# Making VectorE's order by hand in the first stage of a four-layer graph network, with an earlier adjacency load and GpSimd additions cut into tiles

## The chip, the cores and the metric

The kernel runs on one core of one Trainium2 chip. The metric is device time in microseconds (us) of one execution. Times of the kernel before: 2691.99, 2691.94, 2691.20, 2691.12 and 2691.70 us, median 2691.7. One further execution was recorded by the hardware profiler.

## What is computed

Input x is 128 graphs of 64 nodes with 256 features, float32; adj is one 64x64 matrix for all graphs. Four layers follow each other; each ends with a layer norm over the features of x plus the layer's output.

```python
# layer 0: three products with (adj * adj), weights 256->512->1024->256
h = relu(einsum('nm,bmh->bnh', adj*adj, x @ W1))
h = relu(einsum('nm,bmh->bnh', adj*adj, h @ W2))
x = layernorm(x + einsum('nm,bmh->bnh', adj*adj, h @ W3))
# layer 1: features turned into the eigenvectors U of the normalised Laplacian
deg = sum(A, 0) + sum(A, 1) - diagonal(A)
_, U = eigh(rsqrt(deg)[:, None] * (diag(deg) - A) * rsqrt(deg)[None, :])
x = layernorm(x + U @ (relu((U.T @ x) @ W1 + b1) @ W2 + b2))
# layer 2: two graph convolutions, then LSTMs over windows of 1, 2, 3, 4 nodes
x = layernorm(x + lstm_windows(relu(adj @ (relu(adj @ (x @ Wg0 + bg0)) @ Wg1 + bg1))))
# layer 3: attention with the graph as a mask
h = x @ W + b_lin
s = einsum('bnd,bmd->bnm', h, h) * adj
x = layernorm(x + softmax(where(s == 0, -1e16, s)) @ h + b)
```

## The kernel before

The 8192 rows of x lie in SBUF as the tile X, 64 tiles of 128 rows (two graphs each) by 256. The adjacency stands twice on the diagonal of a 128x128 tile (ad2), so that one product mixes two graphs. Its transpose is adT2, the transposed square sqT2.

**First stage (up to about 983 us of the profiled execution).** Two things run at once:

- layer0(g), for 32 steps g, each a pair of row tiles: products with sqT2, W1, W2 and W3 (lines 590-630). A step ends with one 128x512 product (L628, seen in the profile as ps<-s,sqT), the residual addition on VectorE (L629) and rows_norm (L444): statistics on VectorE (L452, L453), reciprocal root on GpSimd (L454, L455), application on VectorE (L457). Two steps are in flight at a time.
- eigen (L40-433), one long generator that computes U for the 64x64 matrix: setup (L84-124), 62 Householder reflectors (L135-178), a tridiagonal stage (L181-267), six bisection passes (L272-291), two recurrences (L300-307), eigenvectors and their signs (to L433). Nearly all of it is small VectorE work; a few products and square roots go to TensorE and ScalarE.

All TensorE products write PSUM tiles from one pool of five (psa, tag "ps"), each released when its reader has read it.

**The order of work.** The functions are generators. Each `yield` hands over a due time on a planned clock now[0], in us, that advances by a fixed cost per product (L580). In eigen, after(n, turns) adds 0.21 us for each of n VectorE operations and 0.6 for each turn over ScalarE, and returns that time plus 0.3. The loop at L638-654 always goes on with the first stream that is due, eigen ahead of the steps. In the block `tc.manual_schedule(engines={PE})` the TensorE queue takes exactly the order in which the loop issues; the order of VectorE, ScalarE, GpSimd and of the DMA queues is made by the framework's own scheduler from its estimates. Every engine works through its queue in order: an instruction that waits holds all behind it.

In one reflector (L135-178) VectorE computes the norm of the rest of a row (L142-145), ScalarE its root (L146), VectorE the reflection vector v (L147-152); TensorE multiplies v and a unit vector with AQ (L156, L157); VectorE then makes the scalars (L158-170), the next row (L172, L173) and the updates of AQ (L174-177).

**Loads.** SP's queue loads W1, the two diagonal blocks of ad2, W2, X tiles 2-3, W3, the rest of X, then smaller weights. ScalarE's queue loads X tiles 0 and 1, a64 (the adjacency for eigen) and eig_c (seven 64x64 constant matrices, the identity among them). GpSimd's queue loads four bias rows broadcast to all partitions (wide).

**Second stage.** Layers 1 to 3 run for 16 groups of four row tiles, three groups in flight, with TensorE's order again made by the loop (L930-946) from due times such as CELL, the time from the last product of an LSTM step to its state (by the number of columns: 256, 168 or 128). GpSimd adds bias rows to X in layer 1 (L721) and layer 3 (L863), each in one instruction over 128x1024, and reorders the LSTM output (L840). The recurrent products appear as ps<-hs,whh, the input products as ps<-w,wih, and layer 1's product with the eigenvectors as ps<-ut,v.

Of the kernel before, what the change touches and what calls it, by code (L numbers as in the profile page):

```python
# [15 lines left out]
N = 64  # L16
# [23 lines left out]
def eigen(tc, stack, a, cst, u2, ut2, now):  # L40
# [25 lines left out]
    eye = cst[:, CONSTS.index("eye"), :]  # L66
# [17 lines left out]
    yield 4.0  # L84
# [22 lines left out]
    dl = sb([N, 1], "c6")  # L107
    V.tensor_sub(dl, deg, dia)
    m = sb([N, N], "m")
    V.tensor_scalar(m, s2, -0.5, None, op0=ALU.mult)  # L110
    V.tensor_mul(m, m, C["off"])
    V.scalar_tensor_tensor(m, C["eye"], dl, m, op0=ALU.mult, op1=ALU.add)
# [21 lines left out]
    after(1)  # L134
    for i in range(N - 2):  # L135
# [10 lines left out]
        S.activation(sq, ss, AF.Sqrt)  # L146
        V.tensor_scalar(g0, rest, 0.0, -1.0, op0=ALU.is_gt, op1=ALU.mult)  # L147
# [6 lines left out]
        yield after(21, 0.5)  # L154
# [19 lines left out]
        V.scalar_tensor_tensor(qt, vt, c2, pt, op0=ALU.mult, op1=ALU.add)  # L174
        V.scalar_tensor_tensor(AQ[:, 0, j:], qr[:, j:], vt, AQ[:, 0, j:], op0=ALU.mult, op1=ALU.add)
        V.scalar_tensor_tensor(AQ[:, 0, j:], xr[:, j:], qt, AQ[:, 0, j:], op0=ALU.mult, op1=ALU.add)
        V.scalar_tensor_tensor(AQ[:, 1, :], pq[:, 1, :], vt, AQ[:, 1, :], op0=ALU.mult, op1=ALU.add)
        xr = nx

# [264 lines left out]
def rows_norm(tc, pool, x, half):  # L444

    nc = tc.nc
    n = x.shape[1]
    st = pool.tile([P, n, 6], F32, name="ln_st")
    mv = pool.tile([P, n, 2], F32, name="ln_mv")
    rs = pool.tile([P, n], F32, name="ln_rs")  # L450
    for t in range(n):
        nc.vector.bn_stats(st[:, t, :], x[:, t, :])  # L452
        nc.vector.bn_aggr(mv[:, t, :], st[:, t, :])  # L453
    nc.gpsimd.tensor_scalar(rs, mv[:, :, 1], EPS, None, op0=ALU.add)  # L454
    nc.gpsimd.tensor_tensor(rs, rs, half[:, :n], ALU.pow)  # L455
    for t in range(n):
        nc.vector.tensor_scalar(x[:, t, :], x[:, t, :], mv[:, t, 0:1], rs[:, t:t + 1],  # L457
                                op0=ALU.subtract, op1=ALU.mult)


@with_exitstack
def kernel(
# [57 lines left out]
    for h in range(2):  # L520
        hs = slice(h * N, (h + 1) * N)
        nc.sync.dma_start(ad2[hs, hs], adj)
    for t in range(2):
        nc.scalar.dma_start(X[:, t, :], x_t[:, t, :])
    aw1 = load(wa, "aw1", a_w1, "(k p) f -> p k f", [P, 2, 512], p=P)
    nc.scalar.dma_start(a64, adj)
    nc.scalar.dma_start(eig_c, consts)
# [4 lines left out]
    nc.sync.dma_start(X[:, 2:4, :], x_t[:, 2:4, :])  # L532
    aw3 = load(wa, "aw3", a_w3, "(k p) f -> p k f", [P, 8, D], p=P)
    for t in range(4, NT, 2):
        nc.sync.dma_start(X[:, t:t + 2, :], x_t[:, t:t + 2, :])
    for h in range(2):
        nc.sync.dma_start(adst[h * N:(h + 1) * N, :], adj)
# [23 lines left out]
    for name, src in (("b_b1", b_b1), ("b_b2", b_b2), ("c_b0", c_b0), ("d_b", d_b)):  # L561
        wide[name] = keep.tile([P, src.shape[0]], F32, name=f"wide_{name}")
        nc.gpsimd.dma_start(wide[name], src.partition_broadcast(P))
# [5 lines left out]

    pt = tl(psa, [P, 512], "ps")  # L570
    PE.transpose(pt[:, :P], ad2, ident)
    V.tensor_copy(adT2, pt[:, :P])
    V.tensor_mul(sqT2, adT2, adT2)
# [16 lines left out]
    def layer0(g):  # L590
# [37 lines left out]
        mm(p, sqT2, s3)  # L628
        V.tensor_add(xs, p, xs)  # L629
        rows_norm(tc, small, xs, half)  # L630

    todo = [layer0(g) for g in range(NT // 2)]
    eig = [0.0, eigen(tc, phase_a, a64, eig_c, u2, ut2, now)]
    going = []
    with tc.manual_schedule(engines={mybir.EngineType.PE}):
# [45 lines left out]
    CELL = {256: 2.6, 168: 2.2, 128: 1.9}  # L683
# [35 lines left out]
    def layer1(xs):  # L719
        a = yield from mixed(xs, u2, (now[0], now[0]))  # L720
        nc.gpsimd.tensor_tensor(xs, xs, ub2.unsqueeze(1).to_broadcast([P, 4, D]), ALU.add)  # L721
# [131 lines left out]
    def layer3(xs, g, ready):  # L853
# [9 lines left out]
        nc.gpsimd.tensor_tensor(xs, xs, wide["d_b"].unsqueeze(1).to_broadcast([P, 4, D]), ALU.add)  # L863
# [125 lines left out]
```

## Time and profile before

| | |
|---|---|
| median of five executions | 2691.7 us |
| the profiled execution | 2691.99 us, its span 2690.2 us |
| granted TensorE clock, mean | 0.985 |
| TensorE products, busy | 2585.8 us (96%) |
| TensorE weight loads, busy | 2260.6 us (84%) |
| VectorE / ScalarE / GpSimd, busy | 1345.2 / 1030.0 / 240.5 us |
| first product of layer 0 | starts at 9.51 us |
| last product of the first stage's steps | starts at 982.24 us |
| reflectors, first and last product read (L166) | 37.8 and 391.5 us |
| bisection passes, first and last start (L276) | 408.3 and 622.7 us |
| end of eigen | 792 us |
| one group of the second stage, in its middle | 103.45 us |

The span runs from the first to the last instruction. A busy row counts the time in which an engine had an instruction in execution. "Idle before" and "waits" name, for the time in which an engine had nothing to do, the instruction whose end let it go on; they are inferred from semaphore events. PSUM tiles are named ps in all lines, so a wait of TensorE for "DVE X L629" is a wait until that addition has read its tile. A float32 product shows as two matmul instructions, so counts are twice those of the code. The granted clock is TensorE's, 1.00 or 0.50 of full speed in this trace.

### The profile page before, as it was taken

The numbers are of one execution on the slowest core, as the hardware profiler recorded it, in microseconds if no ns is written. First come the engines' busy times: TensorE is split into PE (matmuls) and PEld (weight loads), VectorE is DVE, ScalarE is ACT, GpSimd is POOL, SyncE is SP. The second block draws the span as 40 slices with busy tenths as digits, with TensorE's granted clock in tenths as the row PEclk, the third lists the DMA queues.
The fourth block names the chain that finished last, engine by engine and source line by source line (L and its number), as shares of the span: only waits on it lengthen the run. The fifth ranks groups of instructions, "written<-read, shape, count | busy, mean of one in ns | idle before, by whom it ended". The sixth has DMA issues, their size and how long they took to land.

```text
span 2690.2 us, 39840 instructions
## 1 busy us (share of the span) xinstructions
PE 2585.8 (96%) x15384; PEld 2260.6 (84%) x15384; DVE 1345.2 (50%) x5277; ACT 1030.0 (38%) x2526; POOL 240.5 (9%) x336
## 2 busy tenths in 40 slices
PE   7999999999999999999999999999999999999995
PEld 5888887777788887998898898998998988978993
DVE  4777768888510123335445445444444444453345
ACT  2222222222222224454544544445445444445442
POOL 0000000000000010102101101101101011010002
PEclk9999999999999999999999999999999999999997
DMA  8000000000000010000000000000000000000000
GB/s 270 1 1 1 1 1 1 1 1 1 1 1 0 0 48 0 1 9 9 1 9 9 1 9 9 1 9 9 1 9 9 1 9 9 1 9 1 1 1 24
DMA packets 24414, 32.19 MB, mean 12 GB/s; under 512 B 2352, under 2 KB 21040, under 8 KB 24224
## 3 DMA queue, kind: packets, MB, share of 16 engines
q1 hardware_dynamic: 23536, 28.68, 3.2%
q8 instruction: 121, 1.98, 0.3%
q0 software_dynamic: 176, 0.46, 0.1%
q10 hardware_dynamic: 512, 0.51, 0.1%
q14 instruction: 69, 0.57, 0.1%
HBM read 21.25 MB, written 8.39 MB: 11 GB/s over the span
## 4 chain that ended last, share of the span: by engine, by line
PE 50%; DVE 3%; ACT 2%; POOL 1%; issue 1%; POOLq 0%; DVEq 0%; ACTq 0%
PE ps L579 48%; PE ps L686 1%; DVE X L457 1%; POOL ln_rs L455 1%; DVE ln_st L452 1%; DVE X L848 1%; ACT gates L785 1%; PE ps L877 1%; ACT L785 0%; ACT L890 0%; ACT att L890 0%; POOL ln_rs L454 0%; DVE ln_mv L453 0%; DVE hs L795 0%; DVE X L915 0%
## 5 line engine op out<-in xcount | busy, mean ns | idle before, releaser
L579 PE MATMUL ps<-w,wih 128*128 128x128 f32 (+2 forms) x4992 | 891.1, 319 | 1.5 <-ACT w L587 0.7
L579 PEld LDWEIGHTS ps<-w,wih 128*128 128x128 f32 x4992 | 763.1, 191 | 49.3 <-issue 7.2
L785 ACT ACTIVATE gates<-ps,cbi 128x128 f32<-128x128 f32 (+2 forms) x1248 | 499.1, 409 | 533.2 <-PE ps L579 524.7
L579 PE MATMUL ps<-hs,whh 128*128 128x128 f32 (+2 forms) x3072 | 540.5, 303 | 14.3 <-DVE hs L795 14.3
L579 PEld LDWEIGHTS ps<-hs,whh 128*128 128x128 f32 x3072 | 452.3, 191 | 42.2 <-DVE hs L795 19.0
L579 PE MATMUL ps<-m,aw 128*128 128x256 f32 x2048 | 457.0, 381 | 4.7 <-DVE X L629 4.7
L579 PEld LDWEIGHTS ps<-m,aw 128*128 128x128 f32 x2048 | 386.9, 191 | 67.1 <-issue 11.0
L587 ACT ACTIVATE h<-ps 128x256 f32<-128x256 f32 (+1 forms) x320 | 136.2, 426 | 446.4 <-PE ps L579 446.4
L579 PE MATMUL ps<-aw,h 128*128 128x256 f32 x1024 | 229.4, 380 | 0.0
L579 PEld LDWEIGHTS ps<-aw,h 128*128 128x128 f32 x1024 | 193.1, 190 | 36.7 <-issue 12.2
L790 DVE TENSOR_TENSOR gates<-gates 128x256 f32<-128x256 f32 (+2 forms) x256 | 89.8, 351 | 211.5 <-ACT gates L785 211.3
L454 POOL TENSOR_SCALAR ln_rs<-ln_mv 128x2 f32<-128x2 f32 x128 | 31.1, 243 | 1486.5 <-DVE ln_mv L453 1284.3
L457 DVE TENSOR_SCALAR X<-X,ln_mv,ln_rs 128x256 f32<-128x256 f32 x256 | 104.2, 448 | 108.9 <-POOL ln_rs L455 108.9
L793 ACT ACTIVATE gates<-c 128x128 f32<-128x128 f32 (+2 forms) x288 | 98.1, 341 | 106.8 <-DVE c L792 92.5
L804 DVE TENSOR_TENSOR w<-gates 128x256 f32<-128x256 f32 (+2 forms) x160 | 73.9, 467 | 126.5 <-PE ps L579 81.5
L579 PE MATMUL ps<-aw,m 128*128 128x512 f32 x256 | 127.6, 622 | 0.0
L629 DVE TENSOR_TENSOR X<-ps,X 128x512 f32<-128x512 f32 x32 | 21.6, 676 | 208.7 <-PE ps L579 208.7
L789 DVE TENSOR_TENSOR c<-c,gates 128x128 f32<-128x128 f32 (+2 forms) x192 | 65.6, 342 | 113.0 <-ACT gates L785 111.1
L795 DVE TENSOR_TENSOR hs<-gates 128x128 f32<-128x128 f32 (+2 forms) x192 | 63.5, 331 | 95.4 <-ACT gates L793 74.8
L840 POOL COPY w<-w 128x512 f32<-128x512 f32 x32 | 35.6, 1112 | 791.1 <-DVE w L804 791.1
L598 ACT COPY m<-ps 128x256 f32<-128x256 f32 x192 | 71.3, 373 | 71.2 <-PE ps L579 62.6
L280 DVE RECIPROCAL br<-Q 64x16 f32<-64x16 f32 x378 | 92.4, 244 | 12.4
(325 smaller groups left out, 2693.0 us busy)
## 6 DMA issues: line engine op xcount, KB each, us to landing
out_dram<-X SPq DMA_DIRECT2D x32, 256.0 KB, 2.1
X<-in_x_dram SPq DMA_DIRECT2D x31, 256.0 KB, 6.0
wih<-in_c_ih_dram SPq DMA_DIRECT2D x4, 1024.0 KB, 8.0
aw<-in_a_w_dram SPq DMA_DIRECT2D x3, 1024.0 KB, 12.3
whh<-in_c_hh_dram SPq DMA_DIRECT2D x3, 1024.0 KB, 5.3
aw<-in_a_w_dram SPq DMA_DIRECT2D x1, 512.0 KB, 4.7
cw<-in_c_w_dram SPq DMA_DIRECT2D x2, 256.0 KB, 4.4
X<-in_x_dram ACTq DMA_DIRECT2D x2, 128.0 KB, 4.1
```

The lines of the kernel that those rows point to most:

```text
L280: V.reciprocal(r, Q[:, k - 1, :])
L457: nc.vector.tensor_scalar(x[:, t, :], x[:, t, :], mv[:, t, 0:1], rs[:, t:t + 1], op0=ALU.subtract, op1=ALU.mult)
L579: PE.matmul(out, lhsT, rhs, start=start, stop=stop)
L587: S.activation(dst, src, AF.Relu)
L598: S.copy(dst[:, c, :], p[:, :2 * P])
L785: S.activation(gate[q][:, h, :], pp, AF.Tanh if q == "g" else AF.Sigmoid, bias=bias[:, j:j + 1])
L789: V.tensor_mul(c[:, h, :], c[:, h, :], gate["f"][:, h, :])
L790: V.tensor_mul(to, gate["i"][:, h, :], gate["g"][:, h, :])
L793: S.activation(gate["i"][:, h, :], c[:, h, :] if p > 1 else to, AF.Tanh)
L795: V.tensor_mul(new[:, h, :], gate["o"][:, h, :], gate["i"][:, h, :])
L804: V.tensor_mul(hT[:, h, slice(first + p - 1, first + nw * p, p), :], gate["o"][:, h, :].rearrange("p (w b) -> p w b", b=8), gate["i"][:, h ...
L840: nc.gpsimd.tensor_copy(as3(hb[:, k, :], 8), hT[:, k, :, :].rearrange("p n b -> p b n"))
```

## The change

1. In the first stage VectorE's queue follows the loop too: `manual_schedule` names PE and DVE, and the transpose of ad2 with the making of adT2 and sqT2 stands inside the block.
2. rows_norm becomes a generator norm_parts in two parts, with a `yield` between GpSimd's reciprocal root and VectorE's application. In layer0 the addition follows 0.4 us of planned time after its product, the application 3.5 us after the statistics.
3. In a reflector the updates of AQ are kept in a list and issued in the next reflector, after its square root has been issued. The due time of the next product is after(20) instead of after(21, 0.5).
4. In eigen's setup the diagonal is no longer taken out of m by a mask: deg takes the place of dl. The identity comes from the tile ident instead of the loaded constants, and eigen's first due time is 2.0 instead of 4.0.
5. The adjacency is loaded first, on ScalarE's queue; X tiles 0 and 1 move to SP's, X tiles 2-3 ahead of W2; eig_c moves behind X, and the broadcast bias rows move from GpSimd's queue to SP's.
6. GpSimd's two additions are issued as four instructions over 128x256.
7. CELL for 256 columns is 3.3 instead of 2.6.

```diff
@@ eigen, setup
-    dl = sb([N, 1], "c6")
-    V.tensor_sub(dl, deg, dia)
     m = sb([N, N], "m")
     V.tensor_scalar(m, s2, -0.5, None, op0=ALU.mult)
-    V.tensor_mul(m, m, C["off"])
-    V.scalar_tensor_tensor(m, C["eye"], dl, m, op0=ALU.mult, op1=ALU.add)
+    V.scalar_tensor_tensor(m, C["eye"], deg, m, op0=ALU.mult, op1=ALU.add)
@@ eigen, reflectors
+    late = []
     for i in range(N - 2):
...
         S.activation(sq, ss, AF.Sqrt)
+        for update in late:
+            update()
...
-        yield after(21, 0.5)
+        yield after(20)
...
-        V.scalar_tensor_tensor(qt, vt, c2, pt, op0=ALU.mult, op1=ALU.add)
-        V.scalar_tensor_tensor(AQ[:, 0, j:], qr[:, j:], vt, AQ[:, 0, j:], op0=ALU.mult, op1=ALU.add)
-        V.scalar_tensor_tensor(AQ[:, 0, j:], xr[:, j:], qt, AQ[:, 0, j:], op0=ALU.mult, op1=ALU.add)
-        V.scalar_tensor_tensor(AQ[:, 1, :], pq[:, 1, :], vt, AQ[:, 1, :], op0=ALU.mult, op1=ALU.add)
+        def update_a(qt=qt, vt=vt, c2=c2, pt=pt, qr=qr, xr=xr, j=j):
+            V.scalar_tensor_tensor(qt, vt, c2, pt, op0=ALU.mult, op1=ALU.add)
+            V.scalar_tensor_tensor(AQ[:, 0, j:], qr[:, j:], vt, AQ[:, 0, j:], op0=ALU.mult, op1=ALU.add)
+            V.scalar_tensor_tensor(AQ[:, 0, j:], xr[:, j:], qt, AQ[:, 0, j:], op0=ALU.mult, op1=ALU.add)
+        def update_q(pq=pq, vt=vt):
+            V.scalar_tensor_tensor(AQ[:, 1, :], pq[:, 1, :], vt, AQ[:, 1, :], op0=ALU.mult, op1=ALU.add)
+        late = [update_a, update_q]
@@ norm
-def rows_norm(tc, pool, x, half):
+def norm_parts(tc, pool, x, half):
...
     nc.gpsimd.tensor_tensor(rs, rs, half[:, :n], ALU.pow)
+    yield
     for t in range(n):
         nc.vector.tensor_scalar(x[:, t, :], x[:, t, :], mv[:, t, 0:1], rs[:, t:t + 1],
@@ loads
-        nc.sync.dma_start(ad2[hs, hs], adj)
+        nc.scalar.dma_start(ad2[hs, hs], adj)
+    nc.scalar.dma_start(a64, adj)
     for t in range(2):
-        nc.scalar.dma_start(X[:, t, :], x_t[:, t, :])
+        nc.sync.dma_start(X[:, t, :], x_t[:, t, :])
     aw1 = load(wa, "aw1", a_w1, "(k p) f -> p k f", [P, 2, 512], p=P)
-    nc.scalar.dma_start(a64, adj)
-    nc.scalar.dma_start(eig_c, consts)
+    nc.sync.dma_start(X[:, 2:4, :], x_t[:, 2:4, :])
...
+    nc.sync.dma_start(eig_c, consts)
...
-        nc.gpsimd.dma_start(wide[name], src.partition_broadcast(P))
+        nc.sync.dma_start(wide[name], src.partition_broadcast(P))
@@ layer0 and its loop
         mm(p, sqT2, s3)
+        yield now[0] + 0.4
         V.tensor_add(xs, p, xs)
-        rows_norm(tc, small, xs, half)
+        for _ in norm_parts(tc, small, xs, half):
+            yield now[0] + 3.5
...
-    with tc.manual_schedule(engines={mybir.EngineType.PE}):
+    with tc.manual_schedule(engines={mybir.EngineType.PE, mybir.EngineType.DVE}):
+        pt = tl(psa, [P, 512], "ps")
+        PE.transpose(pt[:, :P], ad2, ident)
+        V.tensor_copy(adT2, pt[:, :P])
+        V.tensor_mul(sqT2, adT2, adT2)
@@ second stage
-    CELL = {256: 2.6, 168: 2.2, 128: 1.9}
+    CELL = {256: 3.3, 168: 2.2, 128: 1.9}
...
-        nc.gpsimd.tensor_tensor(xs, xs, ub2.unsqueeze(1).to_broadcast([P, 4, D]), ALU.add)
+        for t in range(4):
+            nc.gpsimd.tensor_tensor(xs[:, t, :], xs[:, t, :], ub2, ALU.add)
```

The addition of d_b in layer 3 is cut in the same way. The new queues place things as follows. TensorE's instructions are the same in number, in a partly different order. On VectorE the scaling of the bias row c_b0 (L660 before) and the sum of the LSTM biases (L661 before), which the code issues after the loop and whose operands are loaded early, stand inside the first stage, among the instructions of the fifth and sixth reflector; on ScalarE's queue a64 is issued ahead of the two blocks of ad2.

## The prediction

> **What bounds the kernel now.** First the page's busy times in 40 slices of 67.3 us.
>
> ```profile
> PE   7999999999999999999999999999999999999995
> DVE  4777768888510123335445445444444444453345
> PEclk9999999999999999999999999999999999999997
> ```
>
> TensorE is the bound: 2585.8 of 2690.2 us busy, and only the first and the last slice are visibly thin. So the change can be worth only what TensorE waits, plus what its clock loses. VectorE is nearly full in slices 6 to 9 (0-based; 404 to 673 us), inside the first stage. Second, TensorE's waits, up to 960 us (the first stage) and from 960 to 2400 us. Columns: total us, times, longest.
>
> ```profile
> PE ps L579 <- DVE X L629: 26.1, 6, 6.4
> PE ps L571 <- DMA ad<-in_adj_dram: 7.5, 1, 7.5
> PE ps L579 <- DMA X<-in_x_dram: 5.9, 1, 5.9
> PE pa L75 <- DVE dm L114: 2.1, 1, 2.1
> ...
> PE ps L579 <- DVE hs L795: 14.3, 10, 1.4
> PE ps L579 <- DVE w L710: 10.9, 4, 4.1
> ```
>
> 26.1 us are waits for the residual add L629, which frees a PSUM tile; 15.5 us lie at the start. Third, the timeline of VectorE and TensorE around one such wait (start, us, engine, line).
>
> ```profile
> 446.94 1.02 PE L579 MATMUL ps<-s,sqT 128*128 128x512 f32 x2
> 451.62 0.24 DVE L280 RECIPROCAL br<-Q 64x16 f32<-64x16 f32 x1
> 452.16 0.24 DVE L280 RECIPROCAL br<-Q 64x16 f32<-64x16 f32 x1
> 453.13 0.68 DVE L629 TENSOR_TENSOR X<-ps,X 128x512 f32<-128x512 f32 x1
> 453.86 1.46 PE L579 MATMUL ps<-sqT,h 128*128 128x128 f32 x8 [4.11 <-DVE X L629]
> ```
>
> The product to be added was ready at 447.96; the add starts 5.17 us later, because bisection steps (one pair L280, L281 per 0.54 us) stand ahead of it. So an add may be 1.06 us late before TensorE waits. Read the same way, the adds from the thirteenth to the twenty-second are late by 1.6, 5.2, 2.6, 6.1, 3.3, 8.0, 4.1, 6.9, 3.3 and 8.0 us; before and after they are at most 1.0 late. Fourth, stretches (PE, PEld, DVE, ACT, POOL busy, granted clock).
>
> ```profile
> 454.60:458.00 3.40, 3.40 (x8) 1.85 (x8) 2.52 (x12) 0.74 (x2) 0.93 (x2) 0.50 0.00 0
> 450.40:622.70 172.30, 159.09 (x723) 130.46 (x724) 150.65 (x579) 38.45 (x94) 5.56 (x12) 0.97 0.00 1
> 875.90:931.30 55.40, 55.40 (x263) 45.66 (x262) 4.79 (x14) 14.03 (x34) 1.85 (x4) 1.00 0.00 1
> ```
>
> After the wait the clock is 0.50 for 3.4 us. The same holds at 516.0, 580.9 (3.4 us each), 638.9 and 703.8 (6.8 and 6.7): half of 23.7, 11.9 us, is lost. In the second row VectorE waits for nothing but 0.7 us per normalisation; it is full. The third row is two steps (pairs of tiles) without eigenwork: 55.4 us. Last, the beginning of the second stage, and one of its groups.
>
> ```profile
> 986.28 4.71 POOL L721 TENSOR_TENSOR X<-X,wide_b_b 128x1024 f32<-128x1024 f32 x2
> 986.30 4.84 DVE L457 TENSOR_SCALAR X<-X,ln_mv,ln_rs 128x256 f32<-128x256 f32 x2 [1.13 <-POOL ln_rs L455]
> 991.79 6.45 PE L579 MATMUL ps<-bw,w 128*128 128x128 f32 x32 [3.81 <-DVE w L710]
> ...
> 1756.88 0.70 PE L579 MATMUL ps<-hs,whh 128*128 128x256 f32 x2 [1.43 <-DVE hs L795]
> 1770.37 1.05 PE L579 MATMUL ps<-ut,v 128*128 128x128 f32 x8
> ```
>
> Two L457 take 4.84 us instead of 0.73 (933-964 us) for as long as GpSimd's additions run; the copies L710 stand behind them and TensorE behind those.
>
> **The change, term by term.**
>
> *Start.* The first product with the second layer's weights (ps<-m,aw) starts at 33.75; what shortens the way to it?
> (a) The adjacency is issued first on ScalarE's queue (0.73, the block-diagonal's second half near 1.8) instead of behind 0.5 MB on SP. The adjacency loads took 5.1 to 5.3 us to land, X on ScalarE's queue 4.1: ready at 5.9 to 6.9 against 7.46. I take 6.5: 1.0.
> (b) X tiles 2-3 now follow 0.75 MB instead of 3.4 MB. 2.0 MB had landed by 10 us (204 GB/s), and they are needed at 6.5 + 2.05 (transpose to first product, as now) + 2.08 = 10.6: the wait of 5.9 goes (3, if they come at 13.5).
> (c) The wait of 2.1 for dm: transpose L86 to dm is 4.25 us; two operations go (0.14, 0.22 us) and the row product L81 (0.22), done early until now, comes in: 4.1. The new TensorE order puts eight 128x512 products (3.5 us) under it: saves 1.5.
> (d) From 9.51 to 33.75 TensorE is busy 16.2 us with work that at its later pace (0.112, 0.432 us) is 11.6. With fewer holes I give back 2 of 4.6 (0 to 4).
> Against it: the scaling of c_b0 (L660) now waits for a load that moved to SP behind all of X; in the new VectorE queue it stands in the fifth reflector, at about 50 us, and the cbi sum nine instructions later. SP issued cbi at 43.8, landing 4.0 later; four 0.5 us issues and the constants' come before it now: 47 to 52. The next product that needs a reflector is 5 us off while its chain takes 3.7: cover 1.5. I charge 0.4 (0 to 4). The constants' load moved behind X is first needed after the reflectors, past 380 us; the LSTM weights, 2 us later, past 1030; GpSimd loses four issues that nothing waited for. Start: 1.0 + 5.9 + 1.5 + 2.0 - 0.4 = 10.0 (4 to 13).
>
> A page of the Trainium skill speaks against (a): "Trainium Kernel Development and Optimization", Key Constraints, says that SP, ScalarE and GpSimd queues share the same 16 DMA engines and that another issuing queue only saves issue time. The trace neither confirms nor denies it (5.1 on SP against 4.1 and 5.3 on ScalarE's); by that page (a) is 0.5 and the sum 0.5 us higher.
>
> *Bisection.* VectorE's queue now follows the planner, and L629 stands where TensorE's order has it, but VectorE's work stays. From the thirteenth to the twentieth add the new queue holds 311 pairs (0.542: 168.6), five pass ends (L284 1.95, L276 1.25, L287 1.25, small ones 1.07: 27.6) and seven add-and-norm bodies (2.1: 14.7): 210.9 us. The old queue between the same adds holds 321 pairs, 216.3, and 4.7 of waits for GpSimd, 221.0; the trace took 217.3 (423.7 to 640.9), so rows overstate by 1.7%: 207.3 is left, with no wait, since 3.5 us lie between the two halves of the norm. TensorE's seven steps take 4 x 25.9 + 3 x 29.5 = 192.1 (850 to 931 us). It must therefore still lose 15.2, less what an add may be late: 1.06 now, some 1.3 more where two 128x512 products follow the product in the new order, 2.4. So 12.8 stay, any half clock being part of it, against 26.1 + 11.9 = 38.0. The recurrence L303-L305 is spread out (at most 32 steps between two adds, 25 us, below the 26 of a step): no wait there. Gain 25 (12 if VectorE's rows are 5% dearer in the new mix, 38 if the lag never builds up).
>
> TensorE: Matmul & The Clock Gate, Part 1, has the clock fall after an idle window of about 3.4 us. The trace shows it also after 2.2 us (2384-2386 us, then 0.50 for 3.35) and never after 1.43; by the page the remaining waits, each below 2.4, would all be at full clock, by the row the last may cost 1.7.
>
> *Reflectors.* The late updates stand under ScalarE's square root (0.2 us, idle 0.3 around it); four instructions leave the chain of 3.7 us from the product to v. TensorE needs v every 5.8 us and waited 0.8 in 62: nothing gained.
>
> *Start of the second stage.* 128x1024 takes 2.36; a 128x2 GpSimd operation takes 0.22, so a quarter costs 0.59 to 0.75. If VectorE gets in between two of them, each L457 waits for one piece: 2 x (0.7 + 0.4) instead of 4.84 saves 2.6, but one piece now stands before each half of the norm's GpSimd work, minus 1.3. With half of the 3.4 lost by 0.50 clock at 990.5: 3 (0 to 7).
>
> *CELL 3.3.* The new order of TensorE's queue puts ut,v (eight instructions, 0.89) ahead of hs in every group, whose input is long ready: the ten waits of 1.43 become 0.54: 8.9 (0, if the copy L735 comes before ScalarE's gates; 14 at most).
>
> *Last group and tail.* At 2382 one L457 pair takes 2.82 behind GpSimd, TensorE waits 2.2 and loses 1.7 by the clock: 2 (0 to 3.9). In the tail GpSimd's 2.39 stretches L883 from 0.43 to 2.45, and 2.35 lie on the chain of waits before ln_rs, now two pieces: 2 + 1, less shifts: 3 (-2 to 6).
>
> Sum 10 + 25 + 3 + 8.9 + 2 + 3 = 51.9. The profiled execution took 2692.0 (span 2690.2 and 1.8 around it; 0.3 above the median of 2691.7): 2640.
>
> **Rivals.**
> *VectorE stays the bound of the middle.* For: it is full from 450 to 665, its work unchanged. Only the order's excess goes, and each remaining wait brings its half clock: the gain there is 5 at most, 2660.
> *The lag never builds up.* For: bodies no longer wait for GpSimd; against: 207 against 192. All 38 go: 2627.
> *Edits that do not do what they say.* X tiles late (3 of 5.9), ut,v's copy delays hs (0 of 8.9): 2640 + 11.8 = 2652.
> *Slower: reflectors late.* VectorE's fixed order keeps the chain behind an add that waits for TensorE, while the due time is cut from 4.71 to 4.2 us. Lateness is paid 62 times: 0.84 us eats the whole gain, 0.93 is 0.2% slower, 1.0 gives 2702. For: any stall is at once TensorE's. Against: 5.8 less 3.7, and even an add body of 2.1 fits between.
>
> **How the numbers follow.** Forecast 2640, its own span 2630 to 2650: 0.54. VectorE bound 0.13, lag gone 0.14, edits idle 0.10, slower 0.06, near nothing 0.03. 0.2% is 5.4 us, about what this kernel's measurement can tell from no change. Below 2686.3: 0.91; within: 0.03; above: 0.06. From 2620 (lag gone, and the upper bounds of the start) to 2667 holds over 8 in 10.
>
> **What would show it.** ps<-m,aw near 23.4 us, no wait for X; adds L629's successor at most 4 us late, TensorE's waits for them summing to about 13; ut,v just ahead of hs and that wait 0.5; a pair of L457 near 2 us at the second stage's start. Wrong: waits of TensorE for reflectors (v) in sum over 5 us, or a wait for c_b0's load above 3.

## The result, and the profile after

The changed kernel takes 2697.4 us (median of 25 executions, 2694.9 to 2702.4), the kernel before on the same chips 2691.4 (45 executions): a ratio of 1.0023, 95% interval 1.0018 to 1.0029. It is slower by 6 us; the forecast was 2640. The profiled execution of the changed kernel has a span of 2694.3 us.

Its page, part 2, 40 slices of 67.4 us:

```profile
PE   8999999999999989999999999999999999999996
DVE  6888878888510033444444445445444444453335
PEclk9999999999999999999999999999999999999997
```

The first slice is fuller, as forecast, and so is VectorE in slices 0 to 5, where the reflectors are. TensorE's waits, up to 960 us and from 960 to 2400 us (total, times, longest):

```profile
PE ps L590 <- DVE X L641: 11.5, 7, 2.7
PE pc L76 <- DVE junk L153: 8.7, 10, 1.5
PE ps L652 <- DMA ad<-in_adj_dram: 6.4, 1, 6.4
PE ps L590 <- ACT h L598: 4.7, 10, 0.5
...
PE ps L590 <- DVE w L879: 12.5, 12, 1.1
PE ps L590 <- DVE hs L813: 10.4, 21, 0.5
...
PE ps L703 <- DVE X L468: 5.7, 15, 1.1
```

The waits aimed at did shrink: for the residual add (now L641) 26.1 to 11.5, for hs 14.3 to 10.4 (21 short ones in place of 10), for X from memory 5.9 to none. Others grew or came: for the reflection vector (L153) 8.7 where 0.8 was, for a ReLU (L598, ten times 0.47), for layer 3's copy of the transposed tiles (L879), and for the norm ahead of layer 3's transposes (the L703 row).

Both traces hold 15,107 TensorE instructions into ps, in an order that differs only locally (at three quarters of the places the tiles are the same). The start of the n-th, counted from 0, in one trace less its start in the other shows where time comes and goes (good to 2 to 4 us where the order differs). The first difference column is the changed kernel, the others are three of the experiments below:

```
   n   before at   changed   e13     e15     e12
  200     68.5      -13.0   -13.2   -12.8   -13.2   start
 1600    391.7       +2.8   -10.5   -11.0   -13.2   reflectors done
 3200    773.9      -12.1   -44.7   -45.2   -52.4   eigenwork nearly done
 4000    947.4      -12.9   -45.1   -45.6   -52.0   end of the first stage
 4400   1033.6      -17.0   -50.6   -49.4   -57.4   second stage begun
 6400   1336.9       -9.5   -43.1   -44.9   -57.4   three groups in flight
13200   2368.7       +6.9   -26.7   -46.1   -57.3   last of the steady groups
15106   2681.0       +4.4   -29.3   -48.7   -60.1   last product
```

So the change wins 13 us at the start, gives 15.8 back over the reflectors, wins 14.9 up to the end of the eigenwork where 25 were forecast (read at the 1,700th product instead of the 1,600th, 11.7 are given back and 10.8 won), wins 4 at the stage boundary, and then loses 23.9 in the second stage, which the prediction had winning 8.9.

Four places show how. First the reflectors: TensorE's timeline (start, us) in the changed kernel.

```profile
173.91 0.39 PE L76 MATMUL pc<-AQ,u 128*128 128x128 f32 x2
174.14 0.33 PE L76 MATMUL pc<-AQ,ident 128*128 128x64 f32 x2
174.31 5.40 PE L590 MATMUL ps<-m,aw 128*128 128x256 f32 x24
180.38 0.46 PE L76 MATMUL pc<-AQ,u 128*128 128x128 f32 x2 [0.68 <-DVE junk L153]
```

Over all 62 reflectors, their products start 5.62 to 6.52 us apart before; after, ten times only 4.74 to 4.81 (the first one above follows its forerunner after 4.80), and in nine of the ten cases the next reflector's product then waits 0.29 to 1.46, as above. VectorE needs 4.98 for the loop of a reflector (L159 at 180.80, the next at 185.78, no wait in between). It was 4.55 before: in the old order independent instructions (L175 here) lay between the steps of the chain. VectorE's timeline before:

```profile
190.19 0.21 DVE L170 TENSOR_SCALAR q<-qr,q 128x1 f32<-128x1 f32 x1
190.32 0.24 DVE L172 SCALAR_TENSOR_TENSOR xr<-qr,q,pc 128x36 f32<-128x36 f32 x1
190.47 0.25 DVE L175 SCALAR_TENSOR_TENSOR AQ<-qr,u,AQ 128x37 f32<-128x37 f32 x1
190.64 0.25 DVE L173 SCALAR_TENSOR_TENSOR xr<-xr,q,xr 128x36 f32<-128x36 f32 x1
```

In the changed kernel the steps stand alone:

```profile
182.40 0.25 DVE L170 SCALAR_TENSOR_TENSOR qr<-xr,q,pc 128x36 f32<-128x36 f32 x1
182.69 0.21 DVE L171 TENSOR_SCALAR q<-qr,q 128x1 f32<-128x1 f32 x1
182.82 0.24 DVE L173 SCALAR_TENSOR_TENSOR xr<-qr,q,pc 128x35 f32<-128x35 f32 x1
183.10 0.26 DVE L174 SCALAR_TENSOR_TENSOR xr<-xr,q,xr 128x35 f32<-128x35 f32 x1
183.39 0.20 DVE L141 SCALAR_TENSOR_TENSOR junk<-xr 128x34 f32<-128x34 f32 x1
```

Here a step that needs the one before starts 0.28 or 0.29 after it, one that doesn't 0.13. So the four updates, which before stood in time that the chain spends waiting for itself, now take time of their own. Second, an add in the bisection, in the timeline of all engines:

```profile
447.15 1.88 PE L590 MATMUL ps<-aw,m 128*128 128x512 f32 x4
449.72 1.38 PE L590 MATMUL ps<-sqT,h 128*128 128x128 f32 x10 [0.47 <-ACT h L598]
451.97 0.68 DVE L641 TENSOR_TENSOR X<-ps,X 128x512 f32<-128x512 f32 x1
452.70 0.71 PE L590 MATMUL ps<-sqT,h 128*128 128x128 f32 x4 [1.60 <-DVE X L641]
```

The add's product was done at 447.32; the add is 4.65 late. ps<-sqT,h waits first for its own ReLU, then for the tile that the add frees. Third, two stretches (PE, PEld, DVE, ACT, POOL busy, clock): the bisection, and two steps free of eigenwork.

```profile
449.30:616.90 167.60, 157.14 (x720) 129.54 (x721) 149.38 (x564) 39.53 (x96) 6.62 (x12) 0.98 0.00 1
834.69:890.81 56.12, 55.66 (x263) 45.72 (x262) 5.06 (x14) 14.15 (x34) 1.85 (x4) 1.00 0.00 1
```

TensorE is idle for 10.5 us of the first; before, it was idle for 13.2 of the row shown there. And two steps, nothing but products, take 56.12 where they took 55.40: the wait of 0.47, and the rest in the instructions behind it. Fourth, one group of the second stage, in layer 3:

```profile
1629.59 1.15 DVE L468 TENSOR_SCALAR X<-X,ln_mv,ln_rs 128x256 f32<-128x256 f32 x2 [0.90 <-POOL ln_rs L465]
1629.79 3.26 POOL L882 TENSOR_TENSOR X<-X,wide_d_b 128x256 f32<-128x256 f32 x4 [0.24 <-PE ps L703]
1630.66 1.81 DVE L822 TENSOR_TENSOR w<-gates 128x256 f32<-128x256 f32 x2
1632.40 0.94 DVE L808 TENSOR_TENSOR gates<-gates 128x256 f32<-128x256 f32 x1
1633.26 0.68 DVE L879 COPY w<-ps 128x512 f32<-128x512 f32 x1
1634.09 3.67 PE L590 MATMUL ps<-w,dw 128*128 128x512 f32 x8 [1.12 <-DVE w L879]
```

The pieces of d_b's addition run while the second half of the norm is still applied. The instructions beside them take 1.15, 1.81 and 0.94 us instead of 0.74, 0.76 and 0.42 (the same instructions before); the copy behind them, and TensorE, come late. Before, the same place of a group reads:

```profile
1635.69 0.74 DVE L457 TENSOR_SCALAR X<-X,ln_mv,ln_rs 128x256 f32<-128x256 f32 x2 [0.90 <-POOL ln_rs L455]
1636.34 0.76 DVE L804 TENSOR_TENSOR w<-gates 128x256 f32<-128x256 f32 x2
1637.01 2.65 POOL L863 TENSOR_TENSOR X<-X,wide_d_b 128x1024 f32<-128x1024 f32 x1 [1.35 <-PE ps L686]
1637.35 0.69 DVE L861 COPY w<-ps 128x512 f32<-128x512 f32 x1
1638.33 1.61 DVE L804 TENSOR_TENSOR w<-gates 128x256 f32<-128x256 f32 x1 [0.29 <-ACT gates L785]
1638.49 3.60 PE L579 MATMUL ps<-w,dw 128*128 128x512 f32 x8
```

The whole addition started when all eight transposes were through, with L457 and nearly all of the two L804 behind it, and what it stretched is an L804 behind the copy. The group's period, 103.45 us before, is 105.04.

Two places went as forecast: the beginning of the second stage, where the two L468 took 4.84 and TensorE waited 3.81, and the wait for hs, 1.43 before.

```profile
975.63 1.54 DVE L468 TENSOR_SCALAR X<-X,ln_mv,ln_rs 128x256 f32<-128x256 f32 x2 [2.07 <-POOL ln_rs L465]
977.83 3.84 PE L590 MATMUL ps<-bw,w 128*128 128x128 f32 x32 [1.45 <-DVE w L727]
...
1647.10 1.06 PE L590 MATMUL ps<-ut,v 128*128 128x128 f32 x8
1649.13 0.70 PE L590 MATMUL ps<-hs,whh 128*128 128x256 f32 x2 [0.54 <-DVE hs L813]
```

### The profile page after: what moved, and what is told of

It is laid out like the page before. It is cut to its first block, busy times and chain, and to the rows that moved or that the text cites. A ratio compares the mean times of both kernels' runs of the same rounds, so it can differ in the third digit from the quotient of the medians.

```text
span 2694.3 us, 39973 instructions
## 1 busy us (share of the span) xinstructions
PE 2586.6 (96%) x15384; PEld 2250.0 (84%) x15384; DVE 1391.7 (52%) x5275; ACT 1031.8 (38%) x2526; POOL 255.8 (9%) x428
## 4 chain that ended last, share of the span: by engine, by line
PE 42%; DVE 5%; POOL 3%; ACT 2%; issue 1%; POOLq 0%; DVEq 0%; ACTq 0%
PE ps L590 40%; DVE X L468 2%; POOL ln_rs L465 1%; POOL X L739 1%; PE ps L703 1%; DVE w L822 1%; DVE X L866 1%; DVE ln_st L462 1%; ACT gates L803 1%; ACT L803 1%; ACT L909 1%; POOL ln_rs L464 1%; PE ps L896 0%; DVE hs L813 0%; ACT gates L811 0%
## 5 line engine op out<-in xcount | busy, mean ns | idle before, releaser
L590 PE MATMUL ps<-hs,whh 128*128 128x128 f32 (+2 forms) x3072 | 543.5, 303 | 10.5 <-DVE hs L813 10.4
L598 ACT ACTIVATE h<-ps 128x256 f32<-128x256 f32 (+1 forms) x320 | 136.2, 426 | 449.6 <-PE ps L590 449.2
L808 DVE TENSOR_TENSOR gates<-gates 128x256 f32<-128x256 f32 (+2 forms) x256 | 96.3, 376 | 240.7 <-ACT gates L803 240.4
L468 DVE TENSOR_SCALAR X<-X,ln_mv,ln_rs 128x256 f32<-128x256 f32 x256 | 108.5, 465 | 95.8 <-POOL ln_rs L465 95.8
L822 DVE TENSOR_TENSOR w<-gates 128x256 f32<-128x256 f32 (+2 forms) x160 | 72.4, 458 | 123.1 <-PE ps L590 81.5
L641 DVE TENSOR_TENSOR X<-ps,X 128x512 f32<-128x512 f32 x32 | 21.9, 684 | 212.3 <-PE ps L590 212.3
L590 PE MATMUL ps<-aw,m 128*128 128x512 f32 x256 | 120.9, 595 | 0.0
L462 DVE BATCH_NORM_STATS2 ln_st<-X 128x6 f32<-128x256 f32 x256 | 98.8, 413 | 1.7
```

The source lines that it names most:

```text
L590: PE.matmul(out, lhsT, rhs, start=start, stop=stop)
L598: S.activation(dst, src, AF.Relu)
L808: V.tensor_mul(to, gate["i"][:, h, :], gate["g"][:, h, :])
L822: V.tensor_mul(hT[:, h, slice(first + p - 1, first + nw * p, p), :], gate["o"][:, h, :].rearrange("p (w b) -> p w b", b=8), gate["i"][:, h ...
```

## The experiments

All were timed with the kernel before on the same chip (median 2691.2 to 2692.4 in each set). Ratios are to it, with 95% intervals.

```
kernel                                          median us   ratio (interval)
changed                                          2697.4     1.0023 (1.0018 to 1.0029)
e1  d_b whole                                    2677.8     0.9954 (0.9939 to 0.9969)
e2  d_b by columns                               2674.1     0.9940 (0.9925 to 0.9955)
e3  CELL 2.6                                     2690.5     0.9998 (0.9989 to 1.0008)
e5  both additions whole                         2691.7     1.0003 (0.9993 to 1.0012)
e9  before, CELL 3.3                             2704.2     1.0049 (1.0032 to 1.0066)
e6  e2 + updates between the chain's steps       2669.5     0.9921 (0.9906 to 0.9936)
e7  e2, VectorE's order free                     2687.3     0.9983 (0.9974 to 0.9993)
e8  e2 + bisection planned at 7 x 0.21           2658.7     0.9882 (0.9867 to 0.9896)
e10 e6 + e8 + body split + loads early           2660.1     0.9884 (0.9866 to 0.9902)
e11 e10, CELL 2.6                                2656.7     0.9871 (0.9853 to 0.9888)
e12 e11, place released                          2633.4     0.9788 (0.9773 to 0.9802)
e13 changed, place released                      2663.6     0.9903 (0.9886 to 0.9919)
e15 changed, place released, d_b by columns      2643.0     0.9822 (0.9808 to 0.9835)
e14 e15, CELL 2.6                                2640.5     0.9809 (0.9796 to 0.9822)
```

**d_b whole, and d_b by columns.** Is it the early start that costs, the cutting, or TensorE's new order?

```diff
-        for t in range(4):
-            nc.gpsimd.tensor_tensor(xs[:, t, :], xs[:, t, :], wide["d_b"], ALU.add)
+        nc.gpsimd.tensor_tensor(xs, xs, wide["d_b"].unsqueeze(1).to_broadcast([P, 4, D]), ALU.add)   # e1
+        for t in range(4):                                                                          # e2
+            c = slice(t * 64, (t + 1) * 64)
+            nc.gpsimd.tensor_tensor(xs[:, :, c], xs[:, :, c],
+                                    wide["d_b"][:, c].unsqueeze(1).to_broadcast([P, 4, 64]), ALU.add)
```

> The changed kernel, with the addition of d_b in layer 3 as one GpSimd instruction of 128x1024 again (all else as changed). Theory: a tile's piece may start as soon as that tile is transposed, 3 us before the second half's normalisation is done, and then stretches the VectorE instructions on the way to the copy L879; TensorE loses 1.28 (w<-ps L879) + 0.42 (transposes of X) + 0.07 a group for it. So the period falls from 105.05 to about 103.3 us, and the time from 2697.4 by 11 x 1.77 = 19.5, plus some 3 in the first groups: 2675 (2671 to 2680). Rival: the period is lost by the new order of TensorE's queue (CELL); then the period stays at 105.0 and the time at 2697.

> The changed kernel, with the addition of d_b in four pieces of the same 256 elements, but cut by columns (64 of each tile) instead of by tiles, so that each piece needs all eight transposes. Theory (the early start costs, not the cutting): as with one instruction, 2675 (2671 to 2681), waits for w<-ps L879 below 0.3 a group. Rival (more, shorter GpSimd instructions cost in themselves, by getting in between VectorE's and the norm's): 2692 to 2700.

2677.8 and 2674.1: both in the range of the theory. With pieces that need all eight transposes the same place of a group reads (timeline of e2):

```profile
1622.44 0.73 DVE L468 TENSOR_SCALAR X<-X,ln_mv,ln_rs 128x256 f32<-128x256 f32 x2 [0.91 <-POOL ln_rs L465]
1623.09 0.75 DVE L822 TENSOR_TENSOR w<-gates 128x256 f32<-128x256 f32 x2
1623.64 1.82 POOL L883 TENSOR_TENSOR X<-X,wide_d_b 128x256 f32<-128x256 f32 x2 [1.24 <-PE ps L703]
1623.76 0.42 DVE L808 TENSOR_TENSOR gates<-gates 128x256 f32<-128x256 f32 x1
1624.10 0.68 DVE L879 COPY w<-ps 128x512 f32<-128x512 f32 x1
```

Four pieces of the same size, but 1.2 us after L468 began instead of beside it, and no VectorE instruction on the way to the copy is stretched; TensorE's waits for L879 are gone from 960 to 2400 us, and the period is 103.28. Cutting as such costs nothing; by columns it is even 3.7 us better than whole, most of it at the end of the kernel (from the 14,800th product on it wins 2.7 us, the whole addition loses 0.4). The early start cost 23.3 us.

**CELL, both additions whole, and CELL in the kernel before** (e3: 2.6 in the changed kernel; e5: b_b2's addition whole too; e9: 3.3 in the kernel before, nothing else).

```diff
-    CELL = {256: 2.6, 168: 2.2, 128: 1.9}
+    CELL = {256: 3.3, 168: 2.2, 128: 1.9}   # e9, on the kernel before; e3 is the reverse on the changed one
```

> The changed kernel with CELL for 256 columns at 2.6 again. The changed kernel waits 0.54 instead of 1.43 for hs in the 256-column cell, but 0.73 more for hs at 168 columns, behind ps<-adT,X. Theory: both are this order's work, a net gain of 0.16 a group: undoing it gives 2699 (2696 to 2702), with ten waits of 1.43 back and those at 168 columns gone. Rival: the wait at 168 columns is made by GpSimd's pieces L739; then it stays, and undoing CELL costs the whole 8.9: 2706.

> The changed kernel, with both GpSimd additions (b_b2 and d_b) as one instruction of 128x1024 each again. Theory: the pieces of b_b2 help only where the second stage starts (TensorE's waits there 7.9 before, about 5.5 to 7 after), so against the kernel with d_b alone whole 2 to 4 us are lost: 2678 (2674 to 2683). Rival: the pieces of b_b2 collide with VectorE in each group as those of d_b do (L468 at 1.13 instead of 0.73 beside them); then 3 to 8 us are won: 2669.

> The kernel before with CELL for 256 columns at 3.3 as its only change. Theory from the runs so far: the new order puts ps<-adT,X straight ahead of the 168-column cell and lets b_b2's whole addition collide with the norm there; a wait of 1.43 is traded for others and the first groups lose: with both additions whole the second stage lost 13 us between 1030 and 2370, so 2691.4 + 13 = 2704 (2697 to 2707). Rival (the prediction on record): ut,v hides most of the wait for hs, ten times 0.89: 2682.

e9 hit: 2704.2, and its waits from 960 to 2400 us say why:

```profile
PE ps L579 <- DVE X L457: 9.1, 13, 0.8
PE ps L579 <- DVE hs L795: 6.1, 12, 0.5
```

The wait for hs does fall, from 14.3 to 6.1 us, and the new order pays for it with waits for the norm (L457) in front of ps<-adT,X, which now comes sooner. e3 missed low: 2690.5 where 2699 was expected, 6.9 better than the changed kernel. The steady groups behave as said (0.16 a group); what was underrated are the first groups, where the changed kernel loses 7.5 us between the 4,800th and the 6,400th product and e3 only 0.9. e5 missed both ways of thinking: 2691.7 where 2678 or 2669 was expected. b_b2's pieces are worth 14 us beside CELL 3.3: 3.6 at the stage boundary, 1 in the first groups, 9.4 in the steady groups, since the whole addition delays the norm that ps<-adT,X waits for. So CELL 3.3 lost in every setting tried (11.8 in the kernel before, 6.9 in the changed one, 3.4 in e10, 2.5 in e15), most where the addition it collides with is whole.

**The reflectors' order, VectorE's order as a whole, the bisection's price.** All three on the kernel of e2 (2674.1). e6 also puts three other small instructions of a reflector (sg, g0 and the row product into pt) back where they stood.

```diff
 # e6: between the steps of the chain, as VectorE had them before
+        V.scalar_tensor_tensor(qt, vt, c2, pt, op0=ALU.mult, op1=ALU.add)
         V.tensor_scalar(qi, qr[:, j:j + 1], th, 2.0, op0=ALU.mult, op1=ALU.mult)
         V.scalar_tensor_tensor(nx[:, j + 1:], qr[:, j + 1:], s0, ...)
+        V.scalar_tensor_tensor(AQ[:, 0, j:], qr[:, j:], vt, AQ[:, 0, j:], ...)
         V.scalar_tensor_tensor(nx[:, j + 1:], xr[:, j + 1:], qi, ...)
+        V.scalar_tensor_tensor(AQ[:, 0, j:], xr[:, j:], qt, AQ[:, 0, j:], ...)
+        V.scalar_tensor_tensor(AQ[:, 1, :], pq[:, 1, :], vt, AQ[:, 1, :], ...)
 # e7
-    with tc.manual_schedule(engines={mybir.EngineType.PE, mybir.EngineType.DVE}):
+    with tc.manual_schedule(engines={mybir.EngineType.PE}):
 # e8, bisection
-                yield after(6)
+                yield after(7)
```

> The kernel with d_b cut by columns (2674.1), and in it the reflector's instructions in the order that VectorE had before: the four updates of A and Q between the steps of the chain qr, nx instead of all together under the square root, L164 between L159 and L160. Theory: in the changed kernel dependent instructions stand back to back (0.28 to 0.30 from one start to the next, against 0.13 to 0.17 where an independent one lies between), so taking the updates out shortens nothing and the loop of a reflector is 4.98 us instead of 4.55; an add-and-norm body of 2.1 then makes TensorE wait, whose pace is 5.63. With 4.55 the slack is 1.08 instead of 0.65: waits for v fall from 8.0 to about 4, 2670 (2666 to 2672). Rival: the bodies alone make the waits, wherever the updates stand: 2674, waits still 7 to 8.

> The kernel with d_b cut by columns (2674.1), with TensorE's order alone written out in the first stage; VectorE's is made by the scheduler again (norm in pieces, due times, loads and start as changed). Theory: the fixed order of VectorE is what gained some 20 us in the bisection and lost some 15 at the reflectors; without it both go: 2680 (2674 to 2688), waits for L641 back to 20 to 27, waits for v under 2. Rival: the bisection's gain comes from the norm in two pieces and the due times; then the fixed order only cost, and the time is 2660.

> The kernel with d_b cut by columns (2674.1), with the planner's price of two bisection pairs raised from 6 x 0.21 to 7 x 0.21 us. Theory: VectorE's queue still holds a little more work between two adds than TensorE's steps last (pairs 1.08 us for a planned 1.26, bodies of 2.8 a step not planned at all); with 1.47 planned it keeps up, the waits for L641 (13.2) and the half clock behind them go, and the eigenwork ends some 35 us later, which nothing waits for: 2660 (2656 to 2665). Rival: the lateness isn't made by the plan's price (it comes from the first step of the bisection and is carried along): 2672 to 2675.

All three times lie in the range of their theory: 2669.5, 2687.3, 2658.7. e6's loop is 4.59 us and its waits for v sum to 3.8 instead of 8.0. e7 comes to its time by another way than its theory said. Of the 15.1 us that e2 loses over the reflectors (200th to 1,600th product) 11.5 are still lost, with waits for v of 4.3 where under 2 were expected; the bisection's gain goes whole (14.8 up to the 3,200th product in e2, -1.2 in e7), but not by waits for the add (7.4, where 20 to 27 were expected): TensorE's waits for the bisection's and the recurrence's own steps come instead (longest for L291 4.6, for L315 5.7). Writing out VectorE's order was itself worth 13 us: 16 in the bisection, less 3.6 that it cost over the reflectors, whose loss is in the main not its doing. In e8 TensorE loses almost nothing in the bisection:

```profile
450.00:617.00 167.00, 165.60 (x770) 135.81 (x770) 141.47 (x535) 41.35 (x99) 5.21 (x11) 1.00 0.00 1
```

165.6 of 167.0 us busy at full clock, against 157.1 of 167.6 at 0.98. The plan, then, asks too much of VectorE here; at this point it looked as if its price for a pair of bisection steps were too low.

**Everything together.** e10 adds to e6 and e8 a norm split once more (add, statistics and application in three places), and early small loads; e11 is e10 with CELL 2.6.

```diff
         V.tensor_add(xs, p, xs)
+        yield now[0] + 3.0
         for _ in norm_parts(tc, small, xs, half):
             yield now[0] + 3.5
```

> The changed kernel with all that the runs point to: d_b cut by columns, the updates of A and Q between the steps of the reflector's chain, two bisection pairs planned at 7 x 0.21, the add L641 and the norm's first half on either side of a reflector instead of together, and the small loads (c_b0, cbi, cbh) ahead of the later tiles of X. Theory: the gains add, since they lie in different stretches: 2658.7 - 4.6 (updates) - 2 (body split: waits for v 3.8 to below 2) - 1.5 (loads: VectorE's waits of 0.97 and 0.82 go, TensorE's of 0.83 and 0.66 behind them) = 2650.6 (2647 to 2655). Rival (what TensorE gets earlier here it waits for later, for eigenwork or the transition): 2656 to 2659.

> The same with CELL for 256 columns at 2.6. Theory: with the pieces in place CELL 3.3 gives 0.16 a group, 1.6, and costs some 2.6 in the first groups; without it the time is 1 lower, 2649.6, within 3 of its twin. Rival (the prediction on record): ten times 0.89, 8.9 higher: 2659.

e11 is 3.4 below e10, where 1 was expected, and not 8.9 above. e10 missed its theory: 2660.1, no better than e8 alone. Its waits for v were down to 1.9 us, but the wait of 0.47 for the ReLU had doubled, from 10 times to 20 (9.3 us). The further the norm is cut, the more often it comes: never before the change, 10 times with the norm in two places, 20 times with it in three. That pointed away from prices to the plan's loop: a pair of tiles keeps one of the two places among the steps in flight until its generator ends, and with every `yield` in its norm it ends later. In that time the plan has products of one pair alone, puts a product straight behind the ReLU it needs, or finds nothing due and sets its clock forward (`now[0] = pick[0]`).

**The place released.** A pair gives up its place when its last product is issued.

```diff
         mm(p, sqT2, s3)
+        held[0] -= 1
...
-            while todo and len(going) < 2:
+            while todo and held[0] < 2:
+                held[0] += 1
                 going.append([0.0, todo.pop(0)])
```

> The kernel with all mended and CELL at 2.6 (2656.7), in which a pair of tiles of the first stage gives up its place among the two that the planner runs as soon as its last product is issued, instead of when its norm is. Theory: with the norm in pieces the pair keeps its place for some us in which TensorE has only the other pair, so ps<-sqT,h follows straight behind the products whose ReLU (L586) it needs: a wait of 0.47 and 0.27 more in the next instructions, 0.74 in each of 20 steps, where the kernel before put ps<-s,sqT and the next pair's ps<-sqT,X between. Released, the pair of steps takes 55.4 us instead of 56.9, and the time falls by 20 x 0.74 = 14.8: 2642 (2639 to 2646). Rival (the 0.74 comes of the weights' loading or of ScalarE, not of the order): 2655 to 2658.

> The changed kernel (2697.4) with only that: a pair gives up its place once its last product is issued. There ten steps show the wait of 0.47. Theory: 0.74 is won in each of the four to five steps that are free of eigenwork; in the bisection TensorE waits for VectorE's adds in any case, so there little is won: 2693 (2690 to 2695). Rival: the time saved is lost elsewhere in the stage: 2696 to 2699.

Both gained far more than expected: 2633.4 (-23.3) and 2663.6 (-33.8, from this edit alone). The expectations had counted only the 0.74 us of the ReLU's wait. The waits of e13 up to 960 us:

```profile
PE ps L655 <- DMA ad<-in_adj_dram: 6.5, 1, 6.5
PE ps L590 <- DVE X L644: 3.2, 4, 1.4
...
PE pc L76 <- DVE junk L153: 1.1, 1, 1.1
```

The waits for the ReLU are gone, those for the add (L644 here) are down from 11.5 to 3.2 without any new price, and those for v from 8.7 to 1.1 with the updates still under the root and the loop still long. At the place shown before, e13's TensorE runs:

```profile
174.53 0.38 PE L76 MATMUL pc<-AQ,u 128*128 128x128 f32 x2
174.75 0.33 PE L76 MATMUL pc<-AQ,ident 128*128 128x64 f32 x2
174.92 5.40 PE L590 MATMUL ps<-m,aw 128*128 128x256 f32 x24
180.16 0.38 PE L76 MATMUL pc<-AQ,u 128*128 128x128 f32 x2
```

The reflectors' products are 5.62 us or more apart throughout. The plan's own arithmetic, followed through the kernel's code, gives the size of the fault: its clock was set forward, over time in which it believed TensorE to have nothing, as follows.

```
                 times   sum us   of it up to 400 us   400 to 720 us (planned clock)
before             13      6.6            3.5               0
changed           128     61.7           16.2              21.5
e13                13      8.9            2.0               0
e10               126     98.5           27.6              30.4
```

TensorE was hardly idle then: in the reflectors the plan sets its clock forward by 3.1 us in every two steps, while TensorE shows no wait of note there but those for v (the first for a ReLU comes at 392 us). So eigenwork due by that clock came too soon: reflectors 4.74 to 4.81 us apart, and more bisection steps between two adds (311 pairs of them from the thirteenth to the twentieth add, against 286 in e13 and 250 in e12). e13 shows that undoing this removes the loss; that each single wait comes from a jump was not traced one by one. For the bisection alone the dearer price does as much: between the 1,600th and the 3,200th product e8 wins 34.6 and e13 34.2. Only the place released mends the reflectors too.

**Both faults.** e15 is the changed kernel with the place released and d_b by columns, nothing else; e14 the same with CELL 2.6.

> The changed kernel with the two faults mended and nothing else: the place given up at the last product, and d_b cut by columns. Theory: they lie in different stages and add: 2697.4 - 33.8 - 23.3 = 2640.3 (2637 to 2644). Rival (they overlap, what the first stage gains the second stage's start gives back): 2648 or more.

> The same with CELL for 256 columns at 2.6. Theory: in the runs with all mended CELL 2.6 was 3.4 lower (2656.7 against 2660.1), by the first groups; so 2637 (2634 to 2640). Rival (the prediction on record): 8.9 higher than its twin, 2649.

2643.0 and 2640.5, the second just above its range: the two faults add up within 3 us (33.8 + 23.3 = 57.1 asked, 54.4 got), and CELL 3.3 costs 2.5. That e15, the change without its two faults, lies 3 us from the forecast of 2640 is in part luck: it wins 34.2 in the bisection where 25 were forecast, and loses 3.3 in the steady part of the second stage where 8.9 were to be won. The fastest kernel, e12, runs at 2633.4, 2.1% below the kernel before.

## Why the prediction was wrong

Three steps failed above all. The norm's `yield` in the loop was charged nothing and cost 33.8 us (e13); the d_b pieces in the steady groups were not priced and cost 23.3 (e2); CELL 3.3 was to win 8.9 and lost 2.5 to 11.8 (e14, e11, e3, e9). The measured time is about that of the rival "reflectors late" with its 0.93 us 62 times, but not for that reason: TensorE waits 8.7 us for v in all. That is above the 5 which the prediction had named as a sign of being wrong. Its terms, against the differences at the n-th product:

- *Start: 10.0 forecast, 13.0 measured at the 200th product.* Right in mechanism. The adjacency came at 6.44 (forecast 6.5); but in the other profiles with these queues it came anywhere from 5.86 to 7.66, and with the old queues at 7.46 and 7.08, so part of that 1.0 may be chance. The wait for X went, the wait for dm is 0.45 (0.6 was to stay), the first ps<-m,aw starts at 21.15 (forecast 23.4). The clock stays full for the first 480 us; before, it was halved from 27.9 to 31.3. Against it VectorE waited 0.97 and 0.82 us for the loads of c_b0 and cbh, and TensorE 1.1 behind them, where 0.4 was charged.
- *Reflectors: 0 forecast, 15.8 lost (11.7 at the 1,700th product).* This step failed, on two points. "TensorE needs v every 5.8 us" was read off the old order; the new one asks for it ten times after 4.7 to 4.8. And "four instructions leave the chain of 3.7" held the chain to be the sum of its instructions: its steps wait for each other anyway, the updates had filled the gaps, and without them the loop grew from 4.55 to 4.98. The bad case was named, with a price of 62 times the lateness and a chance of 0.06, but set aside with "even an add body of 2.1 fits between". e13 keeps the long loop and loses 2.7 us over the reflectors, e6 keeps the pace with a loop of 4.59 and loses 9.0: the pace was the larger part.
- *Bisection: 25 forecast; 14.9 from the 1,600th to the 3,200th product.* The mechanism was right (the adds come late by at most 4.7, forecast 4), and the fixed order is what brings it (e7). So, nearly, was the size of what it priced: the waits for the add and half of the half clock (five stretches before, two after) fell from 38.0 to 11.5 + 3.4 = 14.9, where 12.8 were to stay, 23.1 won. The queue did hold the 311 pairs that were counted; from add to add they took 211.4 us, the rows' sum of 210.9 and not the 207.3 left after taking off 1.7%. What the sum lacked are waits of other kinds among the same products: six for the ReLU (2.8), two for L216 of the later eigenwork (2.0, where one of 1.2 for another product stood before), and some us in the instructions behind them. With the fault out (e13) the same stretch wins 34.2, close to the 38 of the rival that the lag never builds up.
- *Nothing was charged for the norm's `yield` in the loop.* It costs 0.7 us in two steps free of eigenwork, and 33.8 in all: by e13 it is the cause of most of the reflectors' loss (13.1 of 15.8) and of what the bisection falls short (19.3). That two steps are in flight at a time was known; the new order of TensorE's queue, in which ps<-sqT,h follows its own ReLU's product directly and two reflectors stand 4.74 us apart, could be read before any run.
- *Start of the second stage: 3 forecast, 4.1 measured.* The mechanism was right: the two L468 take 1.54 us instead of 4.84, and the wait is 1.45 instead of 3.81. But half clock there shrank as well, from 13.7 us to 3.4, of which the term counted only a part; what took some of that back was not traced.
- *CELL: 8.9 forecast, a loss measured.* The order did put ut,v ahead of hs and that wait is 0.54, as said. The step failed in pricing the one wait that goes and not the products that come forward in its stead: ps<-adT,X then waits for the norm, or leaves 0.45 us to wait at the 168-column cell, and 0.16 a group is left of the 0.89.
- *The d_b pieces in the steady groups: not priced at all, 23.3 lost.* GpSimd's pieces were costed at three places where the whole addition was in the way. That a piece needs only its own tile, and so moves up into the norm, was not thought of, though the stretched L457 beside GpSimd was a row of the prediction itself.
- *Last group and tail: 5 forecast, 2.5 measured.* At the last group the pair of L468 did shrink, 2.82 to 1.54, but the wait that was to go stayed (2.24 for 2.22), since two pieces now stand ahead of the norm's GpSimd work; only the half clock behind it went. In the tail the instruction that GpSimd stretched takes 0.83 for 2.45, and the wait behind it 1.26 for 2.87.

The Trainium skill bears on d_b's pieces. In "SBUF — State Buffer", section "SBUF: two separate sides", it says that VectorE and GpSimd share one pair of ports as a lock held for a whole instruction, not by halves. The rows agree: beside the 0.8 us pieces, the instructions with both inputs in SBUF (L822, L808) take 0.9 us each, about as long as a piece, while the copy out of PSUM keeps 0.68 beside a piece in e2 and 0.69 beside the whole addition before. By that rule cutting does not lower the sum of the stalls, it deals them out to more instructions (here 0.41 + 1.05 + 0.52 against the 1.19 of one L804 before); what e2 shows is that the time at which the pieces run decides.

On the clock, "TensorE: Matmul & The Clock Gate", Part 1, has it fall after an idle window of about 3.4 us. Here half clock followed waits of 2.69 (481 us) and of 0.47 + 1.62 (570 to 574 us), but not one of 2.23 (542 us), nor the like pair of 0.47 + 1.60 shown above (449 to 453 us): a wait well below 3.4 can cost 1.7 us, and its length alone does not say whether it will.

## What to carry to other kernels

Where a plan written in software orders several engines, cutting one stream into more steps also changes who holds a place, and so the order on engines that the cut was not about: look at the new order of the bound engine itself (the work between two requests for the late engine's result), not at its old spacing. Cutting an instruction lets its parts start earlier; before doing so, ask what runs on the shared resource at that earlier time. A wait shortened by reordering is paid by whatever moved forward, so price the new neighbours too.

## What was not expected of the hardware

- In the chain shown, VectorE instructions of 128x36 and less start 0.28 or 0.29 us apart when one needs the other, 0.13 to 0.17 when it does not; filling the gaps took the loop of 25 instructions from 4.98 to 4.59 us without removing any (e6).
- Four GpSimd additions of 128x256 take 3.26 us together with VectorE's work beside them, 0.82 each; one of 128x1024 took 2.35 with only a copy out of PSUM beside it. Four pieces of 128x256 cost TensorE 1.8 us a group when they start 0.2 us after the norm's last application begins, and nothing against the whole addition when they start 1.2 us after it (cut by columns).
